# Output projection in four-tile quads: the seven-product scheme nested, 49 small products, in place of seven per pair

## The chip, the cores and the metric

The kernel runs on one core of a Trainium2 chip. The metric is the device time of one execution in microseconds. A core has TensorE (PE; its weight loads are shown apart as PEld), VectorE (DVE), ScalarE (ACT), GpSimd (POOL) and SyncE (SP), which here only issues DMAs. SBUF is the working memory of 128 partitions, PSUM the small memory that TensorE writes into, DRAM the large one behind the DMA engines.

## What is computed

Four layers with a residual each, on x of 64 x 32 rows of 512 (2048 rows, f32): a per-item channel mix, a linear layer with adapters, attention with a paged cache, and a second channel mix. The change lies in the last product of the attention layer and what follows it:

```python
    o = jnp.einsum('bhqk,bkhd->bqhd', probs, v_all)
    o = o.reshape(bsz, seqlen, HQ * D)
    return jnp.einsum('bse,de->bsd', o, Wo)
...
x = x + _L2_cond_ref(x, ...)
x = x + _L3_cond_ref(x, L3_cond_weights, itok_B_0_15)
```

So o is 2048 x 4096, Wo turns it into 2048 x 512, the result is added to x, and then each item's 32 channels are mixed by a 32 x 32 matrix and added.

## The kernel before

The 2048 rows are 16 tiles of 128. The first two layers and the projections of the attention run ahead of the attention itself, which goes through 512 slots: in two groups of four key heads (g), over 16 tiles, 4 items of a tile and 4 heads. In a slot TensorE computes the scores of one head, the products of an earlier head with the values (line 900), and the transposes of its probabilities (line 890); VectorE takes the row extremum (856), a reciprocal and a copy (892), ScalarE the exponential. GpSimd makes a mask per item (`pen`, line 819) and gathers the values. What else a slot does is written down in a plan: `at(slot, where, do, ...)` puts a piece of work on a slot and a place within it, and `slot(i)` runs the places in a fixed order. All queues are in order, and the order on each engine is the order in which the program issues (`manual_schedule`).

The finished o goes to DRAM transposed, one tensor per group and tile: `o_dram[g][t]`, 128 x 16 x 128, contraction index on the partitions (16 chunks of 128 per group).

The output projection uses the scheme that multiplies 2 x 2 blocks with seven products instead of eight. The blocks: rows by pairs of tiles (a1, a2), the contraction by group (1, 2), the columns of Wo by halves of 256. `product` (line 1365) is 16 matmuls with 128 x 128 of o as the weight and 256 columns of `wo` or of a sum of blocks as the moving operand, added up in one PSUM bank. Pair 0 begins during the attention: `fetch_o` loads its four operands on GpSimd's queue, `early_sum` adds them, `third_weights` makes a difference of weights in place, and `early_product` spreads three of its seven products over the slots from `home = n - 33` = 479 on. After the attention (`l3`) the loop over eight pairs does the rest: per pair four loads of 1 MB on SP, four sums of 2048 elements per partition on VectorE, seven products, and additions out of PSUM straight into the rows of x (`x3`, 128 x 512 each), then `mixed`: one matmul of 512 columns with the channel diagonal, an addition and the store. Pair i's mix waits in `waiting` until pair i+1 has begun, except for the last.

Operands of pair i+1 are loaded into other tiles while pair i is computed; the loads wait, in SP's queue, for the products that read those tiles before.

Of the kernel before, what the change touches and what calls it, by code (L numbers as in the profile page):

```python
# [43 lines left out]
P = 128  # L44
# [33 lines left out]
def resid_kernel(  # L78
# [146 lines left out]


    with ExitStack() as l2:
# [921 lines left out]
        early = {}  # L1149
        o_pools = []  # L1150

        def early_tile(name):
            pool, tag = (wpool, "w8") if name == "a11" else (o_pools[0], "a11" if name == "s3" else name)
            early[name] = pool.tile([P, KG * REP, P], F32, name="o_in", tag=tag)

        def fetch_o(name, i):
            if i == 0:
                early_tile(name)
            part = slice(i * KG * REP // 2, (i + 1) * KG * REP // 2)
            g, t = int(name[2]) - 1, int(name[1]) - 1  # L1160
            nc.gpsimd.dma_start(out=early[name][:, part], in_=o_dram[g][t][:, part])

        def early_sum(dst, a, b, op, i, engine=nc.vector):
            if dst not in early:
                early_tile(dst)
            part = slice(i * KG * REP // 2, (i + 1) * KG * REP // 2)
            dst, a, b = [early[name][:, part] for name in (dst, a, b)]
            engine.tensor_tensor(dst, a, b, op)

        def third_weights(k):  # L1170

            dst = w_sb["o", k][:, :, HID // 2 :]
            nc.vector.tensor_tensor(dst, w_sb["o", KG + k][:, :, HID // 2 :], dst, ALU.subtract)

        def early_product(name, operand, group, half, i):
            if i == 0:
                early[name] = ps_m.tile([P, HID], F32, name="proj_ps", tag="m")
            columns = slice(half * HID // 2, (half + 1) * HID // 2)
            nc.tensor.matmul(  # L1179
                early[name][:, : HID // 2],  # L1180
                lhsT=early[operand][:, i, :],
                rhs=w_sb["o", group * KG + i // REP][:, i % REP, columns],
                start=(i == 0),
                stop=(i == KG * REP - 1),
            )

        def early_keep(name):
            ps = early[name]
            tag = {"p1": "w9", "p2": "w10", "p7": "w11"}[name]
            early[name] = wpool.tile([P, HID // 2], F32, name=name, tag=tag)  # L1190
            nc.scalar.copy(early[name], ps[:, : HID // 2])

        home = n - 33
        for name, slots in (
            ("a11", (-1, 0)),
            ("a12", (7, 9)),
            ("a21", (10, 12)),
            ("a22", (13, 15)),
        ):
            for i, w in enumerate(slots):  # L1200
                at(home + w, "store", fetch_o, name, i)
        for what, begins, over in (
            (("p1", "a11", 0, 0), 2, 10),
            (("p2", "a12", 1, 0), 12, 12),
            (("p7", "s3", 0, 1), 24, 12),
        ):
            for i in range(KG * REP):
                at(home + begins + i * over // (KG * REP), "pe", early_product, *what, i)
            at(home + begins + over - 1, "act", early_keep, what[0])
        for k in range(KG):  # L1210
            at(home + 12 + k, "dve", third_weights, k)
        for what, slots in (
            (("s3", "a11", "a21", ALU.subtract), (17, 19)),
            (("a21", "a21", "a22", ALU.add), (21, 22)),
            (("a11", "a21", "a11", ALU.subtract), (24, 26)),
            (("a12", "a12", "a11", ALU.subtract), (28, 30)),
        ):
            for i, w in enumerate(slots):
                if w < 28:
                    at(home + w, "dve", early_sum, *what, i)  # L1220
                else:
                    at(home + w + 2, "pool", early_sum, *what, i, nc.gpsimd)
# [123 lines left out]
    with ExitStack() as l3:  # L1346
        sums = l3.enter_context(tc.tile_pool(name="sums", bufs=1))
        pool = l3.enter_context(tc.tile_pool(name="out", bufs=1))
        psum = l3.enter_context(tc.tile_pool(name="out_ps", bufs=2, space=PSUM))
        HALF = HID // 2  # L1350

        def block(g, half):

            cols = slice(half * HALF, (half + 1) * HALF)
            return [w_sb["o", KG * g + k][:, :, cols] for k in range(KG)]

        def new_block(name):
            w = sums.tile([P, KG, REP, HALF], F32, name=name)
            return [w[:, k] for k in range(KG)]

        def combine(dst, a, b, op):
            for d, p, q in zip(dst, a, b):
                nc.vector.tensor_tensor(d, p, q, op)

        def product(o, w, within=None):
            ps = psum.tile([P, HID], F32, name="out_ps", tag="p", bufs=6)
            for i in range(KG * REP):
                if within and i == KG * REP - REP:
                    within()
                nc.tensor.matmul(  # L1370
                    ps[:, :HALF],
                    lhsT=o[:, i, :],
                    rhs=w[i // REP][:, i % REP, :],
                    start=(i == 0),
                    stop=(i == KG * REP - 1),
                )
            return ps[:, :HALF]

        def add(dst, a, b):
            nc.vector.tensor_tensor(dst, a, b, ALU.add)  # L1380

        w11, w_3, w21, w22 = block(0, 0), block(0, 1), block(1, 0), block(1, 1)
        lo, hi = slice(0, HALF), slice(HALF, HID)

        def mixed(t, x3, diag, cols=slice(0, HID)):

            ps = psum.tile([P, HID], F32, name="mix_ps")[:, cols]
            nc.tensor.matmul(
                ps,
                lhsT=diag.rearrange("p j c -> p (j c)"),  # L1390
                rhs=x3[:, cols],
                start=True,
                stop=True,
            )
            y = pool.tile([P, HID], F32, name="y", bufs=2)[:, cols]
            add(y, ps, x3[:, cols])
            nc.sync.dma_start(out=out[t * P : (t + 1) * P, cols], in_=y)

        same = same_batch(pool)
        with tc.manual_schedule(engines=ENGINES):  # L1400
            waiting = []
            for pair in range(NT // 2):
                t = 2 * pair

                names = ("a11", "a12", "a21", "a22")
                if pair:
                    a11, a12, a21, a22 = [
                        (pool if pair % 2 and name < "a2" else o_pools[0]).tile(
                            [P, KG * REP, P], F32, name="o_in", tag=name
                        )  # L1410
                        for name in names
                    ]
                    for i, o in enumerate((a11, a12, a21, a22)):
                        nc.sync.dma_start(out=o, in_=o_dram[i % 2][t + i // 2])
                else:
                    a11, a12, a21, a22 = [early[name] for name in names]
                x3 = [pool.tile([P, HID], F32, name="x3", bufs=4) for _ in (0, 1)]
                for i in (0, 1):
                    nc.sync.dma_start(out=x3[i], in_=x_dram[t + i])

                if pair:
                    p_1 = product(a11, w11)
                    p1 = pool.tile([P, HALF], F32, name="p1")
                    nc.scalar.copy(p1, p_1)  # L1424
                    s3 = wpool.tile([P, KG * REP, P], F32, name="s3", tag="w8")
                    nc.vector.tensor_tensor(s3, a11, a21, ALU.subtract)


                    add(a21, a21, a22)
                    nc.vector.tensor_tensor(a11, a21, a11, ALU.subtract)  # L1430
                else:
                    p1 = early["p1"]
                    w_1, w_2, w_4 = new_block("w_1"), new_block("w_2"), new_block("w_4")
                    combine(w_2, w_3, w11, ALU.add)
                for at_last in waiting:
                    mixed(*at_last)
                add(x3[0][:, lo], x3[0][:, lo], p1)
                add(x3[0][:, hi], x3[0][:, hi], p1)
                if pair:
                    p_2 = product(a12, w21)  # L1440
                    nc.vector.tensor_tensor(a12, a12, a11, ALU.subtract)
                    p_7 = product(s3, w_3)
                else:
                    p_2, p_7 = early["p2"], early["p7"]
                    combine(w_1, w22, w_2, ALU.subtract)
                    combine(w_4, w21, w_2, ALU.subtract)
# [8 lines left out]
                if last:  # L1455
                    diag = [channel_diagonal(pool, same, w3, t + i) for i in (0, 1)]
# [102 lines left out]
```

## Time and profile before

| | us |
|---|---|
| runs shown: median (lowest, highest) | 2437.52 (2436.01, 2440.16) |
| the profiled execution, its own time | 2439.1 |
| its span, first to last instruction | 2437.3 |
| TensorE busy in it | 2401.4 |
| VectorE, ScalarE, GpSimd busy | 1647.1, 1400.6, 1234.5 |
| first matmul of the last stage (line 1370) | 2053.0 |
| mean granted clock of TensorE | 0.999 |

The profile gives busy time per engine, the busy share in 40 slices of the span (each 61 us, a digit is tenths), the chain of work that ended last, and groups of instructions by line with count, busy time, mean duration in ns, and the idle time of the engine ahead of them with what ended it. An f32 matmul of the program is two matmuls in the trace. Matmuls overlap: their spacing counts, not their length.

### The profile page before, as it was taken

Reading aid. Unit: us, or ns where it says so; the run is one execution under the profiler, and the core shown is the slowest. Engines: PE = TensorE matmul, PEld = TensorE weight load, DVE = VectorE, ACT = ScalarE, POOL = GpSimd, SP = SyncE. Lnnn points to the kernel's source line nnn. Section 1 sums busy time; section 2 is a strip of 40 time slices with the busy share of each in tenths; the row PEclk is TensorE's granted clock in tenths of the full one; section 3 lists DMA queues with packets and bytes.
Section 4 is the critical chain, followed back from the end, with each engine's and each line's share of the span. In section 5 each row is a group of like instructions: output and inputs, shape, how many; then the busy total and the mean of one; then the engine's idle time right before and its main releaser. Section 6 shows DMA issues by size and latency. Waiting matters only on the chain.

```text
span 2437.3 us, 47128 instructions
## 1 busy us (share of the span) xinstructions
PE 2401.4 (99%) x13794; PEld 1865.4 (77%) x13794; DVE 1647.1 (68%) x3554; ACT 1400.6 (57%) x4006; POOL 1234.5 (51%) x1271
## 2 busy tenths in 40 slices
PE   8999999999999999999999999999999999999999
PEld 5657777777777777777777777777777788888887
DVE  6557777777777777787777777777787756333222
ACT  2346777777777777777777777767677763000000
POOL 3336665566565657665665666565556663000000
PEclk9999999999999999999999999999999999999999
DMA  8876667676766677766566666666667874333221
GB/s 275 257 235 188 199 188 204 186 206 184 203 184 203 190 214 241 231 188 194 175 184 176 191 176 184 181 187 182 179 184 225 254 244 144 107 119 122 87 91 58
DMA packets 461199, 452.09 MB, mean 185 GB/s; under 512 B 67744, under 2 KB 384032, under 8 KB 457360
## 3 DMA queue, kind: packets, MB, share of 16 engines
q1 hardware_dynamic: 405104, 269.05, 36.7%
q0 software_dynamic: 55024, 179.25, 25.0%
q8 instruction: 111, 1.82, 0.3%
q14 instruction: 144, 1.18, 0.2%
q10 hardware_dynamic: 816, 0.79, 0.1%
HBM read 380.73 MB, written 76.55 MB: 188 GB/s over the span
## 4 chain that ended last, share of the span: by engine, by line
PE 94%; DMA 2%; DVE 1%; SPq 1%; ACT 1%; issue 1%; POOL 0%; ACTq 0%; DVEq 0%; POOLq 0%
PE proj_ps L664 23%; PE o_ps L900 18%; PE out_ps L1370 15%; PE s_ps L848 10%; PE pT_ps L890 9%; PE s_ps L851 9%; PE head_ps L766 3%; PE l_ps L481 2%; PE o_ps L913 1%; DMA kT<-kT 1%; SPq L804 1%; PE s_ps L883 1%; PE x1T_ps L450 1%; PE proj_ps L1179 1%; DMA o<-oT 1%
## 5 line engine op out<-in xcount | busy, mean ns | idle before, releaser
L105 POOL DMA_INDIRECT v_sb<-v,v_rows x512 | 543.3, 1061 | 361.6 <-PE o_ps L900 248.3
L900 PE MATMUL o_ps<-pT,v_sb 128*128 128x128 f32 x4096 | 624.9, 275 | 3.3 <-DVE pT L892 3.1
L900 PEld LDWEIGHTS o_ps<-pT,v_sb 128*128 128x128 f32 x4096 | 578.0, 191 | 32.2 <-DVE pT L892 5.4
L867 ACT ACTIVATE sm<-sm,top 128x544 f32<-128x544 f32 x512 | 380.8, 744 | 332.8 <-DVE top L856 241.5
L856 DVE CUSTOM_DVE_ANT_0 sm<-s_ps,pen 128x544 f32<-128x544 f32 x512 | 368.9, 721 | 115.4 <-PE s_ps L851 100.0
L873 ACT ACTIVATE sm<-sm,share 128x512 f32<-128x512 f32 x512 | 369.8, 722 | 108.6 <-DVE share L872 71.0
L892 DVE COPY pT<-pT_ps 128x512 f32<-128x512 f32 x512 | 352.9, 689 | 65.5 <-PE pT_ps L890 16.4
L848 PE MATMUL s_ps<-kT,qT 128*128 128x288 f32 x1024 | 334.7, 409 | 4.5 <-DVE top L856 2.7
L890 PE MATMUL pT_ps<-ident,sm 128*128 128x128 f32 x2048 | 310.0, 274 | 4.8 <-ACT qT L778 3.4
L676 DVE TENSOR_TENSOR raw<-proj_ps,raw 128x512 f32<-128x512 f32 x332 | 224.1, 687 | 131.2 <-PE proj_ps L664 118.8
L851 PE MATMUL s_ps<-kT,qT 128*128 128x256 f32 x1024 | 304.7, 379 | 1.3 <-issue 0.7
L848 PEld LDWEIGHTS s_ps<-kT,qT 128*128 128x128 f32 x1024 | 179.2, 190 | 152.4 <-issue 129.9
L819 POOL TENSOR_SCALAR pen<-key_f,seq_f 128x544 f32<-128x544 f32 x128 | 283.7, 2216 | 13.5 <-DMA kT<-kT 2.2
L890 PEld LDWEIGHTS pT_ps<-ident,sm 128*128 128x128 f32 x2048 | 239.3, 142 | 8.7 <-ACT qT L778 4.6
L720 ACT ACTIVATE sq<-raw 128x128 f32<-128x128 f32 x640 | 198.4, 310 | 73.2 <-DVE raw L676 54.6
L851 PEld LDWEIGHTS s_ps<-kT,qT 128*128 128x128 f32 x1024 | 194.4, 190 | 55.7 <-ACT sm L867 1.1
L105 POOL DMA_INDIRECT mix_rows<-in_w,cond_rows x32 | 37.1, 1160 | 343.7 <-DVE mix_diag L170 299.8
L872 DVE RECIPROCAL share<-total 128x1 f32<-128x1 f32 x512 | 83.8, 164 | 179.1 <-ACT sm L867 150.7
L725 POOL TENSOR_SCALAR ss<-ss 128x4 f32<-128x4 f32 x160 | 38.4, 240 | 311.0 <-ACT sq L720 305.1
L1424 ACT COPY p<-out_ps 128x256 f32<-128x256 f32 x7 | 2.6, 372 | 333.1 <-PE out_ps L1370 333.1
L664 PE MATMUL proj_ps<-sum,x 128*128 128x512 f32 x380 | 188.0, 597 | 0.0
L727 POOL TENSOR_TENSOR rstd<-ss,minus_half 128x4 f32<-128x4 f32 x160 | 169.5, 1059 | 13.3
(178 smaller groups left out, 3572.4 us busy)
## 6 DMA issues: line engine op xcount, KB each, us to landing
kT<-kT SPq DMA_DIRECT2D x2048, 64.0 KB
o_in<-o SPq DMA_DIRECT2D x28, 1024.0 KB
o<-oT POOLq DMA_DIRECT2D x68, 256.0 KB
o<-oT SPq DMA_DIRECT2D x58, 256.0 KB
v<-in_kv_cache SPq DMA_DIRECT2D x32, 256.0 KB
kT<-page_rows SPq DMA_DIRECT2D x32, 256.0 KB
vn<-raw SPq DMA_DIRECT2D x32, 256.0 KB
v_sb<-v,v_rows POOLq DMA_INDIRECT x512
```

What stands on the lines that cost most here:

```text
L105: nc.gpsimd.indirect_dma_start(out=dst, out_offset=None, in_=table, in_offset=bass.IndirectOffsetOnAxis(ap=index, axis=0),)
L664: nc.tensor.matmul(self.ps, lhsT=self.pair.x[x][:, c if x == "b" else half.start + c, :], rhs=blocks(self.b)[w][:, c, :], start=(c == 0), ...
L819: nc.gpsimd.tensor_scalar(self.pen, key_f, seq_f[:, self.b : self.b + 1], BIG, ALU.is_ge, ALU.mult)
L848: nc.tensor.matmul(ps[:, first:HID], lhsT=q, rhs=self.kT[:, :n1, k, :], start=True, stop=True)
L851: nc.tensor.matmul(ps[:, HID : first + LA], lhsT=q, rhs=self.kT[:, n1:, k, :], start=True, stop=True)
L856: nc.vector.tensor_tensor_reduce(out=sm, in0=ps[:, first : first + LA], in1=self.pen, scale=1.0, scalar=3e38, op0=ALU.add, op1=ALU.min, ac ...
L867: nc.scalar.activation(sm, sm, AF.Exp, bias=top, scale=-1.0, accum_out=total)
L873: nc.scalar.activation(sm[:, :L], sm[:, :L], AF.Copy, scale=share)
L890: nc.tensor.transpose(ps[:, c, :], self.sm[k][:, c * P : (c + 1) * P], ident)
L892: nc.vector.tensor_copy(pT, ps)
L900: nc.tensor.matmul(o_of[self.s, k][:, self.j, :], lhsT=self.v[c][:, k * D : (k + 1) * D], rhs=self.pT[k][:, c, :], start=(self.j == 0 and ...
L1370: nc.tensor.matmul(ps[:, :HALF], lhsT=o[:, i, :], rhs=w[i // REP][:, i % REP, :], start=(i == 0), stop=(i == KG * REP - 1),)
```

## The change

The seven-product scheme is applied twice. Four tiles make a quad; rows split into two pairs of two tiles, the contraction into two groups of two halves of 8 chunks, the columns into two halves of two quarters of 128. The outer scheme has seven products per quad (called 1 to 7), and each of these is an `Outer`: seven inner products of 8 matmuls with 128 moving columns. That is 49 inner products per quad, 28 outers in all. Signs are arranged so that all weight sums are differences.

- `Outer` holds four operand tiles of 128 x 1024 and makes four sums (`s1` to `s4`) on VectorE. `post` takes each inner product out of PSUM with additions of 128 columns into a result `m` of 2 x 256 columns; the first goes through a copy on ScalarE.
- `accumulate` adds `m`, on GpSimd, into the blocks of the quad's rows (`acc`, 4 x 512 per partition) that need it: 1 to 4 additions of 512 elements.
- Operands come in pieces of 0.5 MB through a ring of 12 tile tags (5 of them open during the attention): `pump` issues the next pending load on SP as soon as the program has released a tag. Outers 1, 2 and 4 use loaded blocks; 7, 5, 6 and 3 use sums of blocks over the whole quad, made by `combine` from two loads, on VectorE or GpSimd.
- There are two rounds over the quads, with different weight blocks in place. Round one does outers 1, 2, 7, 4 and stores the partial rows of quads 0, 1 and 2 back to `x_dram`; quad 3 stays. Then halves of `wo` are loaded again and combined (`load_weights`, `first_weights`, `second_weights`, `weight_sum`), and round two does 5, 6, 3 for quads 3, 0, 1, 2, ending each with the mixes.
- During the attention, outer 1 of quads 0 and 1 is computed whole, and the operands of outer 2 of quad 0 are loaded; `third_weights`, `fourth_weights` and the sums of weights for outers 1 and 2 are made there as well. The other 26 outers run after it.

The core of the diff (in the line numbers of the changed kernel `post` is 358 to 380, `combine` 1576, `accumulate` 1519):

```diff
+    def weight_sum(what, name, engine):
+        w = w_of[what]
+        a, b = {1: ("3", "11"), 2: ("22", "1"), 3: ("22", "3"), 4: ("2", "21")}[name]
+        for k in (0, 1):
+            engine.tensor_tensor(w.part(str(name), k), w.part(a, k), w.part(b, k), ALU.subtract)
...
+            a, op, b = {
+                "s1": ("21", ALU.add, "22"),
+                "s2": ("s1", ALU.subtract, "11"),
+                "s3": ("11", ALU.subtract, "21"),
+                "s4": ("12", ALU.subtract, "s2"),
+            }[what]
...
+            o, w = self.ORDER[p]
+            for i in chunks:
+                nc.tensor.matmul(
+                    self.ps,
+                    lhsT=self.m[o][:, i, :],
+                    rhs=w_of[self.what].part(w, i // REP)[:, i % REP, :],
+                    start=(i == 0),
+                    stop=(i == 2 * REP - 1),
+                )
...
+            elif p == 5:
+                add(self.block(1, 1), ps, self.u3, ALU.add)
+                add(self.block(0, 1), ps, self.block(0, 1), ALU.add)
...
-            ps = psum.tile([P, HID], F32, name="out_ps", tag="p", bufs=6)
-            for i in range(KG * REP):
...
-                nc.tensor.matmul(
-                    ps[:, :HALF],
-                    lhsT=o[:, i, :],
-                    rhs=w[i // REP][:, i % REP, :],
...
+        def bank():
+            return psum.tile([P, HID], F32, name="out_ps", tag="p", bufs=6)
...
+        def accumulate(o, engine):
+            op = ALU.subtract if o.what == 4 else ALU.add
+            for i, j in TARGETS[o.what]:
+                part = acc[o.quad][:, 2 * i : 2 * i + 2, (lo, hi)[j]]
+                engine.tensor_tensor(part, part, o.out, op)
...
+        def combine(dst, key, a, op, b, engine):
+            engine.tensor_tensor(dst.m[key], a.m[key], b.m[key], op)
...
+        def pump():
+            while pending and free_tags:
+                o, key, block = pending.pop(0)
+                o.load(key, nc.sync, block)
...
+            order = [(2, 0), (2, 1), (7, 0), (7, 1), (4, 0), (4, 1)]
+            order += [(w, q) for q in (2, 3) for w in (1, 7, 2, 4)]
+            order += [(w, q) for q in (3, 0, 1, 2) for w in (5, 6, 3)]
...
+                if what == 5:
...
+                    engine = nc.vector if first else nc.gpsimd
+                    for key, w in zip(KEYS, (-10, -8, -5, -4) if first else (-11, -9, -7, -5)):
+                        then(s + w, combine, o, key, o, ALU.add, a22, engine)
...
+                    for key, w in zip(("21", "12", "11", "22"), (-1, -1, 1, 2)):
+                        then(s + w, combine, of[6, q], key, o, ALU.subtract, of[6, q], nc.vector)
+                    for key, w in zip(("21", "12", "11", "22"), (4, 5, 6, 7)):
+                        then(s + w, combine, of[3, q], key, of[3, q], ALU.subtract, of[6, q], nc.gpsimd)
...
+                for name, w in begin.items():
+                    then(s + w, o.sum, name, nc.vector)
+                then(s + 6, accumulate, o, nc.gpsimd)
...
+            for n, o in enumerate(outers):
+                for p in range(7):
...
+                    o.multiply(p, range(8), bank)
+                    o.post(p)
+                    for key in {3: ("11", "21"), 4: ("12",), 6: ("22",)}.get(p, ()):
+                        o.release(key)
+                    for do, args in todo.pop(step, ()):
+                        do(*args)
+                    pump()
```

## The prediction

> **What bounds the kernel now.** I read the page first, then the windows of the last stage, its groups, and timelines of single spots. TensorE is busy for 99% of the span, at a granted clock of 0.999, and the chain that ended last lies on it for 94%. In the last eight slices VectorE falls to 2 or 3 tenths and GpSimd to 0:
>
> ```profile
> PE 2401.4 (99%) x13794; PEld 1865.4 (77%) x13794; DVE 1647.1 (68%) x3554; ACT 1400.6 (57%) x4006; POOL 1234.5 (51%) x1271
> ...
> DVE  6557777777777777787777777777787756333222
> ...
> POOL 3336665566565657665665666565556663000000
> ...
> PE 94%; DMA 2%; DVE 1%; SPq 1%; ACT 1%; issue 1%; POOL 0%; ACTq 0%; DVEq 0%; POOLq 0%
> ```
>
> The table by windows shows the last stage without a gap on TensorE, while VectorE has 15.5 us of work in 50 and GpSimd 1.9 (columns: stretch, its us, then busy us of each engine):
>
> ```profile
> 2100.00:2150.00 50.00, 50.00 (x229) 43.26 (x228) 15.54 (x21) 0.37 (x1) 1.89 (x2) 1.00 0.30 107
> 2150.00:2200.00 50.00, 50.00 (x229) 43.28 (x228) 15.54 (x21) 0.37 (x1) 1.89 (x2) 1.00 0.30 106
> ```
>
> So there the time is the number of matmuls times their spacing. Each f32 matmul of the program is two in the trace. The spacing comes from runs in the timeline: 8 of 128 columns and 75 of 256, each with its own weight load.
>
> ```profile
> 65.27 1.06 PE L450 MATMUL x1T_ps<-mix_diag,x_sb 128*128 128x128 f32 x8
> ...
> 2060.02 16.35 PE L1370 MATMUL out_ps<-w,o_in 128*128 128x256 f32 x75
> ```
>
> With the last one's own length taken off (0.275 and 0.379 us): (1.06-0.275)/7 = 0.112 and (16.35-0.379)/74 = 0.216 us. A program matmul thus costs 0.432 us at 256 columns and 0.223 at 128: slightly over half.
>
> **TensorE's part.** A product of before is 16 matmuls; 848 of them stand after the attention (4 products of pair 0, 7 of each other pair), 848 x 0.432 = 366.3 us. With 16 mixes (512 columns, 2 x 0.43 us each) 13.8, that is 380.1; the trace has 379.6 from the first at 2053.0 to the last end at 2432.6. After the change 26 outer products of 7 x 8 matmuls stand there: 1456 x 0.223 = 324.9, with the mixes 338.7. Gain, were TensorE alone the limit: 379.6 - 338.7 = 40.9 us.
>
> The Trainium skill, TensorE: Matmul & The Clock Gate, "Back-to-back issue gap", speaks against small products: sustained 81 ns at 128 columns against 131 at 512, so that a quarter of the columns costs 0.62 of the time. This trace has 112 against 430 ns, 0.26; by the page's ratio, as an estimate, the gain would be a loss of some 200 us, by the rows it is the 40.9 above, and the rows decide.
>
> **What feeds TensorE afterwards.** An outer product gives TensorE 56 matmuls, 12.5 us. VectorE's and GpSimd's operations come from these rows (last column group: busy us, mean ns):
>
> ```profile
> L1168 DVE TENSOR_TENSOR o_in<-o_in 128x1024 f32<-128x1024 f32 x6 | 7.2, 1208 | 0.0
> L1168 POOL TENSOR_TENSOR o_in<-o_in 128x1024 f32<-128x1024 f32 x2 | 4.7, 2354 | 0.0
> L475 DVE TENSOR_TENSOR hT<-h_ps,lora_mask 128x128 f32<-128x128 f32 x16 | 4.6, 288 | 9.2 <-PE h_ps L465 9.0
> ```
>
> VectorE: 1.213 us for 1024 elements (the other rows of this shape are 1208 to 1217), 0.685 for 512, 0.288 for 128. GpSimd: 2.354 for 1024; 512 is not in the trace and lies on the line from 0.457 at 128 elements (L604) to 2.354, 1.27. By the order of the instructions, the last stage then holds on VectorE 148 sums of 1024, 8 of 512 and 20 small ones, each with both inputs in SBUF, 190.6 us; and some 200 additions out of PSUM, 64 us. GpSimd gets 89 of 512 (accumulate, sums of weights) and 28 of 1024 (combine), 179 us. Each alone fits in 338.7. The question is whether they run side by side. These lines say that they do not:
>
> ```profile
> 1981.29 1.23 DVE L1173 TENSOR_TENSOR wo<-wo,wo 128x1024 f32<-128x1024 f32 x1
> 1981.33 3.15 POOL L819 TENSOR_SCALAR pen<-key_f,seq_f 128x544 f32<-128x544 f32 x1
> ```
> ```profile
> L819 POOL TENSOR_SCALAR pen<-key_f,seq_f x128: 2097/2116/3149, 176.3 to 2019.5; 128x544 f32<-128x544 f32 x128
> ```
> ```profile
> L604 POOL TENSOR_TENSOR rot_q<-rot_q,q_turn x60: 453/582/906, 214.6 to 1860.9; 128x128 f32<-128x128 f32 x60
> ```
> ```profile
> L761 DVE TENSOR_TENSOR rot_a<-rot_a,rot_b x160: 670/691/1112, 83.5 to 1946.6; 128x512 f32<-128x512 f32 x160
> ```
>
> (min/median/max ns.) The mask of GpSimd, 2116 as a rule, took 3149 behind a VectorE sum begun 0.04 us before: 1.03 us late, of 1.19 that they overlapped. The small product doubles to 906, and VectorE's two-input sum goes from 670 to 1112. So whichever comes second waits until the first lets go, about 0.15 us before its end. The Trainium skill, SBUF — State Buffer, "Who interferes with whom", has the same as a rule, and stricter: the second is blocked for the whole instruction; without the 0.15 us the serial sums below apply.
>
> Now three stretches of the last stage (outers counted from 0). For each: VectorE's two-input work, its PSUM work, GpSimd's two-input work, TensorE's.
> - Outers 0 to 3: 26 x 1.213 = 31.5; 27 x 0.288 = 7.8; 30 x 1.27 = 38.1 (8 of it for the two early products); TensorE 50.0. Two-input work in turn 69.6, less 56 x 0.15 61.2; with the PSUM work in line 77.4. Loss 11.2, 19.6 or 27.4.
> - Outers 13 to 16 (change of weights between the rounds): 27 x 1.213 + 8 x 0.685 + 4 x 0.288 = 39.4; 8.1; 23 x 1.27 + 8 x 2.354 = 48.0; TensorE 50.0. In turn 87.4, less 70 x 0.15 76.9; all in line 95.5. Loss 26.9, 37.4 or 45.5.
> - Outers 17 to 25: 46 x 1.213 + 16 x 0.288 = 60.4; 29.9 (83 operations, 17 for the mixes); 18 x 1.27 + 20 x 2.354 = 70.0; TensorE 126.2. In turn 130.4, less 100 x 0.15 115.4; all in line 160.3. Loss 0, 4.2 or 34.1.
>
> Outers 4 to 12 (59.4, 18.1 and 22.9 against 112.5) lose nothing even in line. Together 38.1 at least, 107.0 at most. I take the middle figures of the first two, since six PSUM banks (6 x 1.78 us) let TensorE run ahead of the additions. In the third I go two thirds of the way to the upper end, 24.1: there every addition that frees a bank stands in VectorE's queue behind sums that wait for GpSimd, and two sums of the next outer are due within four products (7 us), so that little slack is left. Sum 81.1.
>
> Of what is queued: behind a waiting sum on VectorE stand the additions that free banks, and TensorE waits for both; behind SP's loads that wait for a free operand tile stand the rows of x and the new weights. ScalarE gets one copy of 128 columns per outer (under the 0.372 us of L1424) and 24 DMAs, and has nothing else: no cost while it idles.
>
> **The end of the attention** (slots 479 on, about 1942 to 2053). TensorE gets 112 matmuls of 0.223 for 48 of 0.432: 25.0 - 20.7 = +4.3. VectorE gets, in 19 slots, 12 operations of 1024, 12 of 512 and 7 additions, 25 us beside 19 x 1.65 of attention, 56 of about 64 us of TensorE's time; GpSimd 4 x 2.354, and 12 loads instead of 8. I take 2 us of stalls, +6 in all; nothing saved on the waits there (10.8 us of 123) would be +4.3, earlier loads out of the way could give -3, no cover left +15. The tail behind the last matmul (4.7 us) is formed alike: 0.
>
> **Sum.** The profiled execution took 2439.1 with a span of 2437.3. 2439.1 - 40.9 + 81.1 + 6 = 2485.3; the median of the runs lies 1.6 lower, so **2484**. Bounds: 2439.1 - 40.9 + 38.1 - 3 = 2433.3 and 2439.1 - 40.9 + 107.0 + 15 = 2520.2; less 1.6, 2432 to 2519.
>
> **Rivals.**
> 1. TensorE stays the bound (faster). If the sums of the two engines run side by side, VectorE's busiest stretch is 47.5 of 50 and GpSimd's 48.0 of 50, and the banks absorb the rest: 2439.1 - 40.9 + 6 - 1.6 = 2402.6. It decides once the stalls stay under 35 us. For it: 15.5 of 50 on VectorE today, and a mask is not delayed by every sum. Against it: 906, 1112 and 3149 above. One in ten.
> 2. The transfers bound it. 124 operand loads of 0.524 MB, 28 rows of x and 12 back, 12 weights and the output are 86 MB. The densest five microseconds moved 379 GB/s: 227 us, hidden. The slices behind moved 205: 420 us, +40.4, with the +6 again about 2484, but with TensorE waiting for DMA, not for VectorE. 7 in 100.
>
> ```profile
> 2060.00:2065.00 5.00, 5.00 (x25) 4.38 (x24) 5.00 (x7) 0.00 (x0) 2.44 (x6) 1.00 0.97 379
> ...
> 2080.00:2085.00 5.00, 5.00 (x25) 4.41 (x24) 2.62 (x2) 0.00 (x0) 0.00 (x0) 1.00 0.60 205
> ```
>
> 3. The loss and the gain cancel (low end of the sums, no stall early): about 2437, no change. 5 in 100.
>
> **Numbers.** Forecast 78 in 100, the rivals 10, 7 and 5. A difference under 0.2% (4.9 us) can't be told from none. Faster 0.10, same 0.05, slower 0.85. Range 2432 to 2520: the bounds, which leave out rival 1 and a little above.
>
> **What would show it.** Right: TensorE busy in 7 to 8 tenths in the last slices, its waits there ended by VectorE, worst around outers 13 to 16; VectorE's sums of 1024 at a mean over 1.3 us, GpSimd's over 2.6. Wrong: sums at 1.21 beside busy GpSimd, TensorE at 9 tenths to the end, or waits put down to DMA. The matmul spacing at 0.112 confirms the first step whatever the rest does.

## The result, and the profile after

The changed kernel took 2495.68 us (median of 4 runs, 2494.70 to 2499.76) against 2436.77 for the kernel before (4 runs): 1.0242 times as long, 95% interval 1.0225 to 1.0260. The profiled execution took 2495.89 with a span of 2494.1.

The page of the changed kernel, with busy times, the slices of the span and the chain's shares:

```profile
PE 2391.5 (96%) x15142; PEld 1896.7 (76%) x15142; DVE 1847.8 (74%) x3788; ACT 1404.3 (56%) x4024; POOL 1472.3 (59%) x1394
...
PE   8999999999999999999999999999999897996787
...
DVE  5567777777777777887877777777777777668766
...
POOL 3346565656566666665565666566566658226774
PEclk9999999999999999999999999999999999998999
...
POOL 2%; PE 2%; DMA 2%; issue 1%; DVE 1%; POOLq 0%; DVEq 0%
```

The last seven slices are the last stage. TensorE's busy time fell by 10 us in all, and yet it is at 6 to 8 tenths in five of them, where it had been at 9. VectorE, at 2 to 6 tenths before, is at 6 to 8; GpSimd, at 0 before but for the first, is at 8 at the start, at 2 in the light part, at 6 and 7 from the change of rounds on and at 4 in the last slice. In one slice the granted clock falls as well. The chain that ended last, before 94% on TensorE, can be followed back for only 8% of the span, and goes from engine to engine there.

The table by windows (stretch, its us, busy us and operations of PE, PEld, DVE, ACT, POOL, then granted clock, DMA share, GB/s):

```profile
2150.00:2200.00 50.00, 50.00 (x449) 49.96 (x449) 32.25 (x49) 1.06 (x4) 14.42 (x8) 1.00 0.72 237
2260.00:2280.00 20.00, 13.72 (x104) 13.18 (x104) 15.65 (x13) 0.22 (x1) 16.15 (x9) 0.91 0.43 155
2280.00:2300.00 20.00, 7.92 (x50) 7.76 (x50) 18.29 (x12) 0.27 (x1) 16.72 (x11) 0.66 0.16 54
...
2350.00:2400.00 50.00, 43.11 (x336) 40.24 (x335) 35.60 (x46) 0.80 (x3) 34.31 (x18) 0.93 0.59 206
```

The first row is the light part of round one: no gap on TensorE. The next two are the change from round one to round two: VectorE and GpSimd are shown as busy for 16 to 18 of 20 us each, in the second one with only 12 and 11 operations; TensorE has 8 us of work there, and DMA moves 54 GB/s. So the transfers are not what is late.

The waits in the last stage (engine, tile and line, releaser; us in all, times, longest):

```profile
POOL acc L1519 <- DVE m L380: 146.9, 23, 17.8
...
PE out_ps L347 <- DVE s L340: 41.7, 11, 12.1
DVE mix_diag L1529 <- DMA mix_rows<-in_w,cond_rows: 35.9, 11, 6.6
```

TensorE waits for VectorE's operand sums. The wait in the last line was in no step of the prediction: VectorE stands 35.9 us for the gathered rows of the mixing matrices. Those gathers go through GpSimd's queue, behind its sums, into a single tile.

The groups (busy us, mean ns, then the idle time before):

```profile
L1519 POOL TENSOR_TENSOR acc<-acc,m 128x512 f32<-128x512 f32 x55 | 101.4, 1865 | 146.9 <-DVE m L380 146.9
...
L1576 POOL TENSOR_TENSOR o_in<-o_in 128x1024 f32<-128x1024 f32 x28 | 65.3, 2350 | 0.2
L340 DVE TENSOR_TENSOR s<-o_in 128x1024 f32<-128x1024 f32 x25 | 57.6, 2305 | 8.2 <-DMA o_in<-o 8.2
L1576 DVE TENSOR_TENSOR o_in<-o_in 128x1024 f32<-128x1024 f32 x36 | 57.4, 1616 | 0.0
```

VectorE's sum of 1024, 1.213 us by itself, has a mean of 1.6 and of 2.3 us in these two groups; GpSimd's of 512, 1.26 by itself, has 1.865. GpSimd's of 1024 has 2.350, its own length: in this kernel it is never the one that waits. The worst spot, from the timeline (start, us, engine):

```profile
2282.44 11.02 DVE L340 TENSOR_TENSOR s<-o_in 128x1024 f32<-128x1024 f32 x1
2283.02 4.63 POOL L1576 TENSOR_TENSOR o_in<-o_in 128x1024 f32<-128x1024 f32 x2
2287.61 2.47 POOL L251 TENSOR_TENSOR sum_w<-wo 128x512 f32<-128x512 f32 x2
2290.05 2.33 POOL L1576 TENSOR_TENSOR o_in<-o_in 128x1024 f32<-128x1024 f32 x1
2293.50 1.23 DVE L340 TENSOR_TENSOR s<-s,o_in 128x1024 f32<-128x1024 f32 x1
...
2294.87 1.41 PE L347 MATMUL out_ps<-sum_w,s 128*128 128x128 f32 x5 [12.08 <-DVE s L340]
```

One sum of VectorE lasts 11.02 us, over five sums of GpSimd one behind the other; it ends 1.1 us after the last of them, and TensorE has waited 12.08 us for it. By the trace it had begun 0.58 us ahead of the first of the five, while GpSimd was still issuing a gather.

By stretches, each outer product counted from its first matmul (outer 4 begins at 2125.3, outer 13 at 2238.1, outer 17 at 2330.5): outers 0 to 3 took 68.6 us, 4 to 12 112.8, 13 to 16 92.5, 17 to 25 160.8, together 434.7 for 338.7 of matmuls.

### The profile page after: what moved, and what is told of

It reads as the page before. It is cut to its first block, busy times and chain, and to the rows that moved or that the text cites. A ratio compares the mean times of both kernels' runs of the same rounds, so it can differ in the third digit from the quotient of the medians.

```text
span 2494.1 us, 50604 instructions
## 1 busy us (share of the span) xinstructions
PE 2391.5 (96%) x15142; PEld 1896.7 (76%) x15142; DVE 1847.8 (74%) x3788; ACT 1404.3 (56%) x4024; POOL 1472.3 (59%) x1394
## 3 DMA queue, kind: packets, MB, share of 16 engines
q14 instruction: 150, 1.23, 0.2%
## 5 line engine op out<-in xcount | busy, mean ns | idle before, releaser
L1006 PE MATMUL s_ps<-kT,qT 128*128 128x256 f32 x1024 | 305.7, 380 | 2.1 <-ACT p_new L1029 1.1
L362 ACT COPY u<-out_ps 128x128 f32<-128x128 f32 x26 | 6.9, 266 | 403.9 <-PE out_ps L347 260.5
L347 PE MATMUL out_ps<-wo,o_in 128*128 128x128 f32 x1664 | 204.7, 281 | 21.2 <-DVE o_in L340 14.6
L347 PEld LDWEIGHTS out_ps<-wo,o_in 128*128 128x128 f32 x1664 | 197.5, 197 | 29.2 <-DVE o_in L340 14.2
L1519 POOL TENSOR_TENSOR acc<-acc,m 128x512 f32<-128x512 f32 x55 | 101.4, 1865 | 146.9 <-DVE m L380 146.9
```

The source lines that it names most:

```text
L347: nc.tensor.matmul(self.ps, lhsT=self.m[o][:, i, :], rhs=w_of[self.what].part(w, i // REP)[:, i % REP, :], start=(i == 0), stop=(i == 2 * ...
L1006: nc.tensor.matmul(ps[:, HID : first + LA], lhsT=q, rhs=self.kT[:, n1:, k, :], start=True, stop=True)
```

## The experiments

Theory A, the prediction's: sums with both inputs in SBUF take turns on VectorE and GpSimd, and TensorE waits for what is late through that. Rival B: the amount of work and the order in the queues are too much, whether the engines share anything or not. Theory C, from the trace after: part of the loss is the late rows. Each run stands beside the kernel before on its own chip; the stage is that of one profiled execution, counted from the first matmul of L347 in it to the last end. All edits are to the code of the last stage. The first row and the four whose name says "all" or "reordered" are medians of 4 to 6 executions; the other seven are a single execution each.

| kernel | us | before, same chip | difference | last stage |
|---|---|---|---|---|
| changed kernel | 2495.68 | 2436.77 | +58.9 | 434.7 |
| GpSimd only writes | 2434.19 | 2432.11 | +2.1 | 370.5 |
| all sums on VectorE | 2447.48 | 2432.11 | +15.4 | 387.1 |
| rows early | 2477.80 | 2432.11 | +45.7 | 420.0 |
| GpSimd's sums broken up | 2502.89 | 2432.11 | +70.8 | 442.8 |
| all on VectorE, rows early | 2466.65 | 2435.18 | +31.5 | 385.7 |
| no sums, rows early | 2425.19 | 2435.18 | -10.0 | 344.5 |
| round one reordered, rows early | 2463.46 | 2435.18 | +28.3 | 379.4 |
| combine on VectorE, rows early | 2465.64 | 2435.18 | +30.5 | 404.0 |
| all on VectorE, reordered | 2443.08 | 2431.95 | +11.1 | 383.0 |
| no sums | 2401.33 | 2431.95 | -30.6 | 343.3 |
| rows early, idle gathers | 2482.06 | 2431.95 | +50.1 | 420.9 |

The kernel before spread over up to 8.5 us on one chip, so differences of a few us between single runs say nothing.

### GpSimd only writes

```diff
+        class WriteOnly:
+            def tensor_tensor(self, out, a, b, op):
+                for _ in (0, 1):
+                    nc.gpsimd.memset(out, 0.0)
+
+        gp = WriteOnly()
...
-                then(s + 6, accumulate, o, nc.gpsimd)
+                then(s + 6, accumulate, o, gp)
```

It leaves out GpSimd's accumulations, combines and weight sums (`gp` stands in all their calls), and writes zeros there.

> GpSimd's 117 sums of the last stage are replaced by two writes of zeros each to the same tiles: the same queue, the same waits for and of it, but no reading of SBUF (the additions into the rows, the combined operands and some sums of weights are left out). Theory A (the two engines' two-input sums exclude each other): all VectorE sums of 1024 fall to 1.21 us, the 76 us that they and the diagonals took over their own length go, and so do most of the 64 us that TensorE waited for VectorE; 2425 to 2455 us. Theory B (VectorE's waits are late operands or its own load, the long durations only show them): 2480 us or more, with the same waits of TensorE.

2434.19, as A has it. GpSimd still had 142.7 us of writing (55.5 + 52.8 + 26.2 + 8.2 in its groups), and VectorE's sums had their own length again (groups of this run):

```profile
L1494 POOL MEMSET o_in<- 128x1024 f32 x56 | 52.8, 955 | 1.6
...
L340 DVE TENSOR_TENSOR s<-o_in 128x1024 f32<-128x1024 f32 x25 | 30.4, 1214 | 8.2 <-DMA o_in<-o 8.2
...
L1583 DVE TENSOR_TENSOR o_in<-o_in 128x1024 f32<-128x1024 f32 x36 | 43.0, 1216 | 1.3 <-DMA o_in<-o 1.0
```

The same 373 operations kept VectorE busy for 231.0 us in the last stage here and 305.7 in the changed kernel: 74.7 us of its busy time there are waiting inside instructions. It is the reading that collides, not the activity. What the run doesn't give is the price of the reading alone: the zeros do not wait for `m` either (146.9 us of GpSimd's waits in the changed kernel), and writing them takes some 36 us less than the 179 forecast for the sums. The Trainium skill, SBUF — State Buffer, "Who interferes with whom", says that a two-input VectorE operation contends with a GpSimd instruction that reads SBUF, and not with one that only writes it, nor does a VectorE operation with one SBUF input outside what the page calls 2-port perf modes. All three show: 1.214 here, and the additions out of PSUM stayed at 0.28 to 0.29 us in every kernel. The page has the second one blocked "for the whole instruction"; in the changed kernel one stayed blocked over five instructions (the 11.02 us above).

### All sums on VectorE

```diff
+        gp = nc.vector
...
-                then(s + 6, accumulate, o, nc.gpsimd)
+                then(s + 6, accumulate, o, gp)
```

So too for the combines and the weight sums.

> All of GpSimd's sums of the last stage go to VectorE. Theory A: nothing is left to share, 255 us of VectorE's work become 255 + 89 x 0.685 + 28 x 1.213 = 350 us at their own length, against 338.7 of TensorE; the last stage takes 350 to 375 us instead of 434.7, in all 2411 to 2436 us. Theory B (VectorE's own load is what TensorE waits for): 95 us more work on it makes it slower than the changed kernel, over 2500 us.

2447.48, 1.0062 times the kernel before (1.0042 to 1.0082). B falls: with more work on the fuller engine the stage shrank from 434.7 to 387.1 us. But A's range is missed too. Every sum ran at its own length (1.21, 0.69). The lengths of all of VectorE's operations add up to 349.2 us, as expected; since in the trace one operation begins a little before the last one ends, VectorE was busy for only 318.8 of the stage, but not evenly. Outers 13 to 15 took 17.9, 22.2 and 17.7 us for 12.5 of matmuls, and outer 0 took 26.8, where it takes 15.6 in the kernel without sums below: the accumulations of the two early products now stand in VectorE's queue between the operand sums that TensorE waits for. The range had been worked out from the sum of VectorE's work; the dense stretches and the order in its queue were not in it.

### Rows early

```diff
-rows_of_mix[t] = pool.tile([P, S], F32, name="mix_rows")
+rows_of_mix[t] = key_f[:, t * S : (t + 1) * S]
...
-then(s - 14 + 3 * a, fetch_mix, q, a)
+then(30 + 8 * q + 2 * a, fetch_mix, q, a)
```

> The 16 gathers of the channel rows for the last mix, which VectorE waited 35.9 us for in the second round behind GpSimd's sums, are issued in the first round, where GpSimd has gaps, into a tile that is free by then. Theory C (the gathers are a cost of their own in the second round): 2455 to 2480 us. Theory A: VectorE's wait moves to the sums behind, which need the same port and the same results of GpSimd; 2485 to 2495 us, and the long sums get longer.

2477.80: C is right about some 13 us against the kernel before (45.7 for 58.9), or 14.7 of the stage. Without the gathers between its sums GpSimd no longer held VectorE out for long either: the longest sum of VectorE fell from 11.02 to 3.4 us. Now the engines alternate, and GpSimd's sums of 1024 wait as well (groups of this run):

```profile
L1576 POOL TENSOR_TENSOR o_in<-o_in 128x1024 f32<-128x1024 f32 x28 | 80.2, 2882 | 5.1 <-DMA o_in<-o 3.8 <-DVE o_in L1576 1.2
...
L340 DVE TENSOR_TENSOR s<-o_in 128x1024 f32<-128x1024 f32 x25 | 37.9, 1516 | 13.0 <-DMA o_in<-o 7.9 <-POOL o_in L1576 5.1
```

### GpSimd's sums broken up

```diff
+            def tensor_tensor(self, out, a, b, op):
+                nc.gpsimd.tensor_tensor(out, a, b, op)
+                for _ in (0, 1, 2):
+                    nc.gpsimd.memset(key_f[:, :S], 0.0)
```

> After each of GpSimd's sums three short writes of 128 x 32 to a tile that nobody reads, some 0.35 us in all, so that its next sum does not follow at once. If GpSimd keeps VectorE out over several sums because its next one stands ready (the 11.0 us sum), the longest VectorE sum falls to 2 to 3 us, and the stage gets 5 to 25 us shorter although GpSimd has 40 us more to do: 2470 to 2490 us. If the long sum waited for something else, it stays above 5 us, and the extra work makes it 2495 to 2530 us.

2502.89. The small writes do let VectorE in, its longest sum is 3.36 us, but the time is no better. GpSimd's queue got longer, and the wait for the rows behind it grew from 35.9 to 48.7 us (waits of this run):

```profile
DVE mix_diag L1538 <- DMA mix_rows<-in_w,cond_rows: 48.7, 11, 15.6
```

VectorE's five groups of sums of 1024 and the diagonals took 236.1 us for 246.8 in the changed kernel. So the long blocks are not the cause by themselves: what VectorE gets back (10.7), the rows lose (12.8).

### All on VectorE with rows early: a trap

Both edits together.

> All sums of the last stage on VectorE, and the rows of the mixing matrices fetched early into memory that lies idle there (the two edits that gave 2447 and 2478 alone). Theory A (with the sums off GpSimd its queue is free, so the gathers are on time anyway): within 4 us of the kernel with the sums alone, 2443 to 2450. Rival C (the late gathers cost their 18 us whatever else stands in GpSimd's queue): 2427 to 2433.

Neither: 2466.65, 1.0134 (1.0117 to 1.0151), 16 us worse against its own before than without the early rows. The timeline at the end of the attention shows why:

```profile
2041.27 0.08 DVE L1011 DVE_READ_ACCUMULATOR2_ANT top<- 128x1 f32 x1
...
2045.61 0.94 POOL L105 DMA_INDIRECT key_f<-in_w,cond_rows  x1 [0.31 <-issue]
2046.86 0.95 POOL L105 DMA_INDIRECT v_sb<-v,v_rows  x1 [0.30 <-issue]
...
2051.19 0.69 DVE L1047 COPY pT<-pT_ps 128x512 f32<-128x512 f32 x1 [9.84 <-remote]
```

With no sums of the last stage left on GpSimd, the sixteen early gathers into the idle memory had been placed ahead of the attention's last four gathers of v. At 1.25 us apiece the sixteen take 20 us; the four begin at 2046.86, for 2031.52 in the kernel with all sums on VectorE, and TensorE fell to half clock for 17.1 us. The last stage, once begun, takes 385.7 us for 387.1: there the rows are worth next to nothing, since nothing stands in GpSimd's queue. What VectorE's 9.84 us ended on the trace doesn't name; that the early rows are the cause follows from the pair of runs without sums below, whose edits differ in nothing else.

### Without the sums: what TensorE alone would give

```diff
+        def same_tile(self, what, engine):
+            self.m[what] = self.m[{"s1": "22", "s2": "22", "s3": "21", "s4": "12"}[what]]
+
+        Outer.sum = same_tile
...
-                part = acc[o.quad][:, 2 * i : 2 * i + 2, (lo, hi)[j]]
-                engine.tensor_tensor(part, part, o.out, op)
+                pass
...
-            engine.tensor_tensor(dst.m[key], a.m[key], b.m[key], op)
+            pass
```

The weight sums stay, on VectorE.

> Leaves out every sum of operands (s1 to s4, combine) and every accumulation of the last stage; loads, matmuls, additions out of PSUM, weight sums and mixes stay. If TensorE is the next limit, as the forecast has it: last stage 339 to 345 us, whole 2393 to 2403, about 35 under the kernel before, and half clock gone with the waits. If the operand loads bind it (rival 2 of the prediction): last stage 400 us or more, 2455 or above, with TensorE's waits put down to DMA.

2425.19, outside both ranges: the trap above, in this kernel too; its last stage was 344.5 us. The same with the rows at their first place:

> Leaves out every sum of operands and every accumulation of the last stage, as the run without sums did, with the rows fetched where they were at first. If the 2425 of that run was the attention's last slots waiting behind sixteen gathers, and the rest TensorE alone: stage 339 to 343 us, whole 2396 to 2404, some 34 under the kernel before. If something else of the change (loads, clock) holds the program there: 2415 or above again.

2401.33, 30.6 under the kernel before, and the stage 343.3 us for 338.7 of matmuls. The tables by windows, in the change of rounds and over the stage (the clock is the third number from the end):

```profile
2250.00:2300.00 50.00, 50.00 (x427) 48.09 (x426) 12.46 (x39) 0.80 (x3) 5.65 (x6) 1.00 0.69 228
```
```profile
2057.00:2397.00 340.00, 336.44 (x2921) 328.89 (x2919) 98.91 (x271) 6.63 (x25) 16.61 (x21) 1.00 0.73 255
```

All the loads, matmuls, PSUM additions and mixes of the change are in it. So transfers and the order of the products cost 4.6 us at most as long as no sum holds up a load; the operand sums and accumulations, with what waits behind them, are the rest of the loss. The pair of runs also prices the trap: 30.6 - 10.0 = 20.6 us.

### Combine alone

```diff
-                    engine = nc.vector if first else nc.gpsimd
+                    engine = nc.vector
...
-                        then(s + w, combine, of[3, q], key, of[3, q], ALU.subtract, of[6, q], nc.gpsimd)
+                        then(s + w, combine, of[3, q], key, of[3, q], ALU.subtract, of[6, q], nc.vector)
```

> As the kernel with early rows (2478), and GpSimd's 28 sums of 1024 (combine) on VectorE; its 89 of 512 stay. Theory by time at the port: 66 of GpSimd's 179 us become 34 on VectorE, the cost falls by about 66/179 of the 30 us between 2478 and the kernel with all sums on VectorE, so 2462 to 2470. Rival, the long GpSimd sums are what holds VectorE out for several in a row: 2446 to 2456.

2465.64 (+30.5, with the rows early alone +45.7), in the range of the theory by time: 16.0 us of the stage for 28 sums of 1024. No operation of VectorE lasted over 2.4 us any more. GpSimd's 89 sums of 512 cost the other 18.3 us to the kernel with all on VectorE (385.7).

### Round one reordered

```diff
-order += [(w, q) for q in (2, 3) for w in (1, 7, 2, 4)]
+order += [(w, q) for ws in ((1, 7), (2, 4)) for q in (2, 3) for w in ws]
...
-then(s + 18, first_weights, k)
+then(s + 17 + k, first_weights, k)
```

The loads of weights and rows, the stores and the other sums of weights are moved to fit.

> All sums on VectorE, rows fetched early, and in round one both products by weights 1 and 7 ahead of those by 2 and 4, so that the first new weights and their sums (4 of 1024, 8 of 512: 10 us of VectorE) move from outers 12 and 13 into 10 and 11, where VectorE has room. Theory: the time over 339 us is VectorE's own excess in the stretches that are fuller than TensorE's; moving 10 us out of the fullest one gives 6 to 10 us against the kernel without the reorder, 2434 to 2441. Rival: that excess is set by when operands come free, not by the sum of the work: within 3 us of it, 2442 to 2448.

2463.46; the trap again, and in this kernel some weights of round two are other numbers (one block is changed ahead of the sum that reads it). The stage took 379.4 us, 6.3 less than the 385.7 without the reorder, the low end of the theory's 6 to 10; the whole time missed its range by the trap. With the rows at their first place and that block in order:

> The kernel with all sums on VectorE (2447 beside 2432), the rows fetched where they were at first (the early fetch had been put ahead of the attention's last gathers on GpSimd's queue, which cost about 20 us there), and round one reordered, so that 10 us of VectorE's weight work leave outers 12 and 13. The last stage with the reorder took 6 to 7 us less from outer 0 on in the run before, so 1.0028 to 1.0045 times the kernel before if that carries over (2439 to 2443 beside 2432); if the stage only trades one wait for another, 1.0062 again. Under 1.000 if, without the disturbed start, the clock too is granted in full.

2443.08, 1.0047 times the kernel before (1.0033 to 1.0061), just past the range: 4.1 us of the stage carried over (383.0 for 387.1). Outers 13 to 16 did gain 6.6 (65.6 for 72.2). It is the fastest form of the change found here, though its interval and that of the kernel without the reorder (1.0042 to 1.0082) overlap, and it is still slower than the kernel before. The table by windows tells what is left:

```profile
2250.00:2300.00 50.00, 39.88 (x311) 38.38 (x311) 47.62 (x74) 0.62 (x3) 4.75 (x4) 0.90 0.53 177
2350.00:2400.00 50.00, 47.64 (x388) 44.28 (x388) 45.06 (x67) 0.80 (x3) 5.67 (x4) 1.00 0.65 221
```

With GpSimd out of it, VectorE itself is full in the change of rounds (47.6 of 50) and nearly so in round two (45.1). Of the 44.3 us over the matmuls, 11.4 against the kernel without sums lie in outer 0 alone (27.0 for 15.6), where VectorE stands 5.0 us before a sum of weights and then does eight accumulations of early products between the operand sums. So the order in its queue costs too, and no run here moved these.

### Do gathers in the queue let GpSimd keep VectorE out?

```diff
+        def fetch_idle(q, a):
+            t = 4 * q + a
+            idle = pool.tile([P, S], F32, name="mix_rows")
+            gather(idle, w3, cond_rows[:, t : t + 1])
...
+                    then(30 + 8 * q + 2 * a, fetch_mix, q, a)
+                    then(s - 14 + 3 * a, fetch_idle, q, a)
```

> The kernel with early rows (2478), and the sixteen gathers issued at their old places in GpSimd's queue a second time, into a tile that nobody reads. If a gather ahead is what lets GpSimd keep VectorE out over several sums: sums of 5 to 11 us on VectorE are back, time 2486 to 2496. If the long ones came with the waits for the rows: the longest sum stays at 3.4 us and the time at 2476 to 2484 (sixteen issues of about 1 us on GpSimd).

2482.06 and a stage of 420.9 us for 420.0: the gathers themselves cost the stage next to nothing, so its 13.8 us to the changed kernel are the waits for the rows (by the whole times, each against its own before, 8.8). The time lies in the second theory's range. But VectorE's longest sums are 5.83, 4.70, 4.53 and 4.28 us, neither the 3.4 of the one theory nor the 11 of the other. GpSimd's sums of 1024 are back to a mean of 2.568 (2.882 with no gather between them, 2.350 in the changed kernel). So what decides whether GpSimd keeps VectorE out over several sums or alternates with it stays open.

## Why the prediction was right, point by point

- **Spacing and TensorE's part: right.** In L347 the matmuls at full clock stand 111.7 ns apart (0.112 forecast). The kernel without sums shows the 338.7 as 343.3, and a whole time 30.6 under the kernel before, 2401.33; the price of rival 1, TensorE as the bound, was 2402.6.
- **Taking turns: right**, and shown by the kernel in which GpSimd only writes. The price of one collision was about as read off the mask (1.03 us late behind 1.23): in the kernel with early rows, GpSimd's 2.35 became 3.33 behind a sum of 1.21, 0.98 late. But one sign failed: GpSimd's sums of 1024, forecast at a mean over 2.6, kept 2.350; of its sums only those of 512 waited (1.865 for 1.26). And "whichever comes second waits until the first lets go" doesn't cover the 11.02 us, where VectorE let five sums by.
- **The sum over the stretches: 81.1 forecast, 96.0 measured.** Outers 0 to 3: 18.6 for 19.6. Outers 13 to 16: 42.5 for 37.4, inside the 26.9 to 45.5. Outers 17 to 25: 34.6 for 24.1, just past the 0 to 34.1. Outers 4 to 12: 0.3 where nothing was forecast. The last two stretches hold waits for the rows and half clock, which were not in the sum: with the rows early outers 13 to 16 lose 32.6, with all sums on VectorE 22.2. So the closeness of the whole is in part luck. With the rows on time and the gathers still in the queue (idle gathers) the stage loses 82.2, of which 16.2 are the wider spacing at half clock: some 66 are left for what the 81.1 was meant to hold. The middle figures were too high by about 15, and two terms that the prediction missed, 16.2 and 13.8, came on top. A part of the 15 is that VectorE's operations were summed by their length: in the kernel with all sums on VectorE sums of 1.22 us begin 1.13 to 1.15 us apart.
- **The first missed term: the clock.** 168 of the matmuls in the last stage stand 0.212 us from the next instead of 0.112: 35.7 us where 18.8 would do, 16.9 lost. The granted clock was at half for 58.0 us of the last stage (none before), behind long waits of TensorE (0.66 over the stretch with the 11.02 us sum). In the kernel without sums it is at half nowhere in the stage. The prediction took every wait at its own length.
- **The second: the queue behind GpSimd's sums.** The prediction named what is queued behind VectorE's sums and in SP's queue, but not the sixteen gathers in GpSimd's: 13.8 us of the stage by the idle gathers.
- **"Outers 4 to 12 lose nothing even in line": right** (112.8 us for 112.5). TensorE's first wait of the dense stretch, 1.7 us, comes within outer 13.
- **The attention's end: +6 forecast, +3.6 measured** (the stage's first matmul at 2056.6 for 2053.0), inside its -3 to +15. **The tail:** 2.8 us behind the last matmul for 4.7, -1.9, where 0 was forecast. With the stage's +14.9 these make 10.6, the difference between 2485.3 and the profiled 2495.9. The 379.6 and the 4.7 were read to and from the last matmul of L1370 (2432.6); the last mix ended at 2433.9, so like for like the stage of before is 380.8, the gain of TensorE alone 42.1 and the tail's change -0.7.
- **Rivals.** Transfers: TensorE waited 3.1 us in all for an operand's load. TensorE as the bound: it would need the sums to cost under 35 us; by the length of the stage they cost 43.8 alone on VectorE (343.3 to 387.1), sharing with GpSimd another 32.9 (to 420.0), and the late rows 14.7 (to 434.7). By the whole times it is 46.0, 30.3 and 13.2.
- **The estimate beside the spacing.** "Some 200 us" of loss by the page's ratio has no working: 0.62 is for a quarter of the columns, and the loss comes out between some 130 and 230 according to how it is put on a half. Nothing in the forecast rests on it.

## What to carry to other kernels

A scheme that trades matmuls for sums can be bounded by the engine that adds: here some 41 us of TensorE were saved, and the sums cost 44 even with VectorE to itself, in the order tried. Moving 117 of them to GpSimd was no relief, since both inputs lie in SBUF: the slower engine holds the faster one for its own, longer time, and everything else in its queue, gathers too, comes late. Work out such a stage by its fullest stretch, not by its mean, and look what an engine's emptied queue lets move ahead.

## What was not expected of the hardware

- GpSimd can hold VectorE out over several of its sums: 11.02 us over five, where one would be 2.35. In the kernel with the rows early the same sums alternate. What decides between the two is open.
- TensorE's clock goes to half behind long waits, so that a wait costs more than its own length: of the 96 us lost, 16.9 are spacing. With all sums on VectorE the stretches at half clock in the last stage are 3.41, 6.83 and 10.24 us long. The Trainium skill, TensorE: Matmul & The Clock Gate, Part 1, has the gate judge activity in windows of 3413 ns and halve the clock after an idle one; these lengths are one, two and three of its windows.
- GpSimd's sum of 512 f32 elements takes 1.26 us alone (estimated at 1.27), its fill of 1024 0.955.
